# Where the coupling net of the last layer runs: after the attention for half-batches, or by pairs of blocks between other work

## The chip, the cores and the metric

The kernel runs on one core of a Trainium2 chip. A core has a matrix engine (TensorE, PE), a vector engine (VectorE, DVE), an activation engine (ScalarE, ACT), a general engine (GpSimd, POOL) and SyncE (SP), which here only starts DMA transfers. Each engine takes its instructions in a fixed order; they meet through semaphores. TensorE reads SBUF and writes PSUM, which has eight banks of 128 x 512 fp32. The metric is the time of one execution in device microseconds.

## The reference, cut to what matters

Four layers run one after the other over 16 sequences of 256 tokens of 128 features. Each layer adds an attention-like part and a feed-forward part, both of the normalised input. The diff touches the feed-forward part of layer 3 and where it stands:

```python
xn = _layernorm(x)                                  # entering layer 3
x = x + attention(xn, Wq, Wk, Wv, Wo) + ffn(xn)     # causal, 16 heads of 8

def ffn(x):
    gf = global_net(x.mean(axis=1))                 # 128-64-32-1, sigmoid
    out = x
    for _ in range(3):
        tf = coupling_net(out)                      # 128-128-64-32-1, exact gelu, sigmoid
        coupling = 0.1 + adaptive_range * (0.7 * gf + 0.3 * tf - 0.5) * 2.0
        out = out + coupling * twist(out)           # swaps quarters of the features, with signs
    return out
```

Layer 2 adds `attention over a window of 3` and a feed-forward part of `silu(x w1) * (x w2)`, two 512 x 512 products with exact gelu, and a 512 x 128 product.

## The kernel before, in words

The tokens are eight blocks of 512 (two sequences each). `X[i]` holds a block with tokens on partitions, `xT[i]` its normalised form with features on partitions. All products are fp32.

**Layer 2** (L1108 to L1193) goes block by block. `window(i)` makes q, k, v and the windowed softmax, with DVE, ACT and POOL doing most of it; eight products a and b give h0; then 16 products of 128x512 for h1 and 16 for h2 (the loop at L1173), and `po`, the 20 small products that come out with tokens on partitions. A scheduler orders this part by what the program says first. While block i is in h1 and h2, `ahead` normalises block i - 1 for layer 3 through `norm_steps` (L175), which takes a step at each `next`. Eight single PSUM banks are in use (`banks(8, 0)`).

**Layer 3's attention** (`attention`, L800, called at L1223) has its order written out by hand for PE, ACT and DVE (L991). It is a pipeline over sequences s = 0 to 17: for sequence s, `maxima` (three steps of scores `sc` and their DVE maxima M); one sequence later `weights` (three steps of exponents E, with the causal part cut by POOL); two later `context` and `divide`. `project` makes the next block's Q, K, V between steps, `shift` turns the maxima (`mT`) and builds Q2, `turn` makes `cT[i]`. PSUM is held as two single banks and three pairs (`banks(2, 3)`). An iterator `beside` is advanced twice or three times per sequence; in layer 3 it is `means` (L1213): it normalises block 7 and then takes the mean of every sequence (`gx`). Layer 1 calls the same function with hooks in its gaps (`dense(s, gap, cT)`).

**The coupling stage** (L1229 to L1420) follows. For a half of four blocks, `first` is the 128-128 product c1 (per block), `second` the 128-64 product c2 (two blocks side by side in the array), `third` the 64-32 product c3 (four blocks side by side), `fourth` the 32-128 product c4, which repeats the scalar coupling over all 128 partitions, and `twists` the product that swaps quarters. DVE and POOL update `xT`. The two halves alternate over three cycles:

```python
                for cyc in (1, 2):
                    first(0, cyc, range(0, 2))
                    third(1, cyc - 1)
                    first(0, cyc, range(2, 4))
                    fourth(1, cyc - 1)
```

For the last cycle of each half, and all of half 0, a second form is kept with tokens on partitions: `columns_of` (L1277) gets the couplings by tiny products `cd`; `finish_first` (L1339) combines them with the kept normalised blocks `xn3` on POOL and DVE; `turn_second` and `finish_second` (L1366) do the last twist of half 1. `attended` (L1325) multiplies `cT[i]` by Wo and adds it to `X[i]`. The eight output transfers leave from the two finish functions.

Of the kernel before, what the change touches and what calls it, by code (L numbers as in the profile page):

```python
# [9 lines left out]
F32 = mybir.dt.float32  # L10
# [8 lines left out]
P = 128  # L19
B, S, D = 16, 256, 128  # L20
NBLK = 8
# [17 lines left out]
PK3 = dict(wq=256, wk=256, wv=128, wo=128, c1=128, c2=64, c3=32, c4=128, cd=4, g1=64, g2=32, g3=128,  # L39
# [12 lines left out]
def program(ctx: ExitStack, tc: tile.TileContext, x, consts, consts0, rows, pk0, w0s, w0e, pk1, pk1i, pk2, pk3, out):  # L52
# [122 lines left out]
    def norm_steps(pool, blocks, layer, into=None):  # L175


        n = len(blocks) * NT
        mv = pool.tile([P, n, 2], F32, tag="mvs", name=f"mv{layer}_{blocks[0]}")
        for k, i in enumerate(blocks):  # L180
            stats(pool, X[i], mv[:, k * NT : (k + 1) * NT, :], f"st{layer}_{i}")
            yield
        r = inv_std(pool, mv, n, f"r{layer}_{blocks[0]}")
        for k, i in enumerate(blocks):
            t = into(i) if into else pool.tile([P, NT, D], F32, tag="xn", name=f"xn{layer}_{i}")
            normalise(t, X[i], mv, r, k * NT)
            yield
            ps = transpose4(t, f"xnT{layer}_{i}")
            nc.scalar.copy(xT[i], ps)
            yield  # L190
# [609 lines left out]
    def attention(ap_, kp_, blocks, w, layer, beside=iter(()), dense=None, keep=NBLK):  # L800
# [190 lines left out]
        with tc.manual_schedule(engines={mybir.EngineType.PE, mybir.EngineType.Activation, mybir.EngineType.DVE}):  # L991
            for _ in project(blocks[0]):
                pass
            coming = iter(())
            turns = []
            for s in range(len(seqs) + 2):
# [3 lines left out]
                for step in range(3):  # L1000
                    if now:
                        maxima(*now, step)
                    if step < 2:
                        next(beside, None)
                    if step == 0 and old:
                        context(*old)
# [88 lines left out]
    xn3p = ctx.enter_context(tc.tile_pool(name="l3n", bufs=1, side="right"))  # L1095
    xn3 = {}

    def kept(i):

        t = xn3[i] = (xn3p if i in HALVES[0] else fp).tile(  # L1100
            [P, NT, D], F32, tag=f"xn{i}" if i in HALVES[0] else "xn", name=f"xn3_{i}"
        )
        return t


    with banks(8, 0), tc.tile_pool(name="l2w", bufs=1) as wp, tc.tile_pool(name="l2", bufs=2) as sp:
# [47 lines left out]
        ahead = iter(())  # L1154
        for blocks in HALVES:
            norm_half(blocks, 2)
            for i in blocks:

                if i > 0:
                    ahead = norm_steps(fp, (i - 1,), 3, kept)  # L1160
                steps = window(i)
                next(steps)
                h0 = sp.tile([P, 4, 512], F32, tag="h0", name=f"h0_{i}")
# [10 lines left out]
                for wn, sn in (("h1", "t1"), ("h2", "t2")):  # L1174
                    for _ in range(2):
                        next(ahead, None)
                    hn = sp.tile([P, 4, 512], F32, tag=wn, name=f"{wn}_{i}")
                    wv = W2[wn].rearrange("p (c o) -> p c o", c=4)
                    for c in range(4):
                        ps = bank(f"{wn}_{i}_{c}")  # L1180
                        for kc in range(4):
                            mm(ps, wv[:, kc, c * P : (c + 1) * P], prev[:, kc, :], kc == 0, kc == 3)
                        nc.scalar.activation(hn[:, c, :], ps, AF.Gelu, scale=W2[sn][:, c : c + 1])  # L1183
# [14 lines left out]
    with tc.tile_pool(name="l3w", bufs=1) as wp:  # L1198

        hb4 = wp.tile([P, 1], F32, tag="hb4", name="hb4")  # L1200
        nc.vector.tensor_scalar(hb4, W3["cb4"], 0.5, None, ALU.mult)
        hg3 = wp.tile([P, 1], F32, tag="hg3", name="hg3")
        nc.vector.tensor_scalar(hg3, W3["gb3"], 0.5, None, ALU.mult)

        c2 = wp.tile([P, 1], F32, tag="c2", name="c2")
        nc.vector.tensor_scalar(c2, W3["ar"], 0.3, None, ALU.mult)
        ar2 = wp.tile([P, 1], F32, tag="ar2", name="ar2")
        nc.vector.tensor_scalar(ar2, W3["ar"], 2.0, None, ALU.mult)

        with banks(2, 3), tc.tile_pool(name="l3a", bufs=2) as sp:  # L1210
            gx = wp.tile([P, B], F32, tag="gx", name="gx")

            def means():  # L1213
                yield from norm_steps(fp, (NBLK - 1,), 3, kept)
                for i in range(NBLK):
                    nc.vector.tensor_reduce(
                        gx[:, 2 * i : 2 * i + 2], xT[i].rearrange("p (b s) -> p b s", b=2), AX.X, ALU.add
                    )
                    yield
                nc.vector.tensor_scalar(gx, gx, 1.0 / S, None, ALU.mult)  # L1220
                yield

            cTs = attention(sp, wp, range(NBLK), W3, 3, means())  # L1223

        with banks(4, 0), tc.tile_pool(name="l3t", bufs=4, space=PSUM, reuse_waits="tile") as tp, \
                tc.tile_pool(name="l3", bufs=2, reuse_waits="tile") as sp:  # L1229
            base = wp.tile([P, B], F32, tag="base", name="base")  # L1230

            def context_net():
                ps = bank("gc1")
                mm(ps[0:64, 0:B], W3["g1"], gx)
                g1 = sp.tile([64, B], F32, tag="g1", name="g1")
                nc.scalar.activation(g1, ps[0:64, 0:B], AF.Gelu, bias=W3["gb1"][0:64])
                ps = bank("gc2")
                mm(ps[0:32, 0:B], W3["g2"][0:64], g1)
                g2 = sp.tile([32, B], F32, tag="g2", name="g2")
                nc.scalar.activation(g2, ps[0:32, 0:B], AF.Gelu, bias=W3["gb2"][0:32])  # L1240
                ps = bank("gc3")
                mm(ps[:, 0:B], W3["g3"][0:32], g2)
                nc.scalar.activation(base, ps[:, 0:B], AF.Tanh, bias=hg3, scale=0.5)

                nc.vector.tensor_scalar(base, base, 0.35, 0.35 + 0.15 - 0.5, ALU.mult, ALU.add)
                nc.vector.tensor_scalar(base, base, ar2, 0.1, ALU.mult, ALU.add)

            h1, h2, h3, tws, olds = {}, {}, {}, {}, {}


            turn = [None, None]

            def first(hf, cyc, ns):
                for n in ns:
                    i = HALVES[hf][n]
                    ps = bank(f"c1_{i}_{cyc}")
                    mm(ps, W3["c1"], xT[i])
                    h1[i] = sp.tile([P, 512], F32, tag="c1", name=f"c1_{i}_{cyc}", bufs=8)
                    nc.scalar.activation(h1[i], ps, AF.Gelu, bias=W3["cb1"])

            def second(hf, cyc):
                for p in range(2):
                    ps = bank(f"c2_{hf}{p}_{cyc}")
                    for n in range(2):
                        mm(ps[64 * n : 64 * n + 64], W3["c2"], h1[HALVES[hf][2 * p + n]])
                    h2[hf, p] = sp.tile([P, 512], F32, tag="c2", name=f"c2_{hf}{p}_{cyc}", bufs=4)
                    nc.scalar.activation(h2[hf, p], ps, AF.Gelu, bias=W3["cb2"])

            def third(hf, cyc):
                ps = bank(f"c3_{hf}_{cyc}")  # L1270
                for n in range(4):
                    r = slice(64 * (n % 2), 64 * (n % 2) + 64)
                    mm(ps[32 * n : 32 * n + 32], W3["c3"][r], h2[hf, n // 2][r])
                h3[hf] = sp.tile([P, 512], F32, tag="c3", name=f"c3_{hf}_{cyc}", bufs=3)
                nc.scalar.activation(h3[hf], ps, AF.Gelu, bias=W3["cb3"])

            def columns_of(hf, cyc):  # L1277
                ps = bank(f"cd_{hf}_{cyc}")
                for t in range(NT):
                    mm(ps[:, 4 * t : 4 * t + 4], h3[hf][:, t * P : (t + 1) * P], W3["cd"])  # L1280
                c = sp.tile([P, 2, 2, 4], F32, tag="cc", name=f"cc_{hf}_{cyc}", bufs=4)
                nc.scalar.activation(c.rearrange("p b t n -> p (b t n)"), ps[:, 0:16], AF.Tanh, bias=hb4, scale=0.5)
                of = base[:, 8 * hf : 8 * hf + 8].rearrange("p (n b) -> p b n", b=2)
                V = nc.vector
                for b in range(2):
                    V.scalar_tensor_tensor(
                        c[:, b], c[:, b], c2, of[:, b].unsqueeze(1).to_broadcast([P, 2, 4]), ALU.mult, ALU.add
                    )
                if cyc == 0 or hf == 1:
                    turn[hf] = (None, c)  # L1290
                    return
                a, b = (sp.tile([P, 2, 2, 4], F32, tag=k, name=f"{k}_{hf}_{cyc}", bufs=4) for k in "ab")
                pa, pb = turn[hf]
                V.tensor_tensor(a, pb, c, ALU.mult)
                if pa is None:
                    V.tensor_scalar(a, a, -1.0, 1.0, ALU.mult, ALU.add)
                    V.tensor_tensor(b, pb, c, ALU.add)
                else:
                    V.tensor_tensor(a, pa, a, ALU.subtract)
                    V.tensor_tensor(b, pa, c, ALU.mult)  # L1300
                    V.tensor_tensor(b, b, pb, ALU.add)
                turn[hf] = (a, b)

            def twists(hf, cyc):

                for n, i in enumerate(HALVES[hf]):
# [269 lines left out]
```

## Time and profile before

| | us |
|---|---|
| three executions | 1379.95, 1381.39 (median), 1388.58 |
| the profiled execution | 1382.97 |
| its span in the profile | 1381.3 |
| TensorE busy in the span | 1261.4 (91%) |
| VectorE busy | 774.8 (56%) |
| ScalarE busy | 573.5 (42%) |
| GpSimd busy | 349.0 (25%) |
| granted TensorE clock, mean | 0.967 of full |

All times below are from the start of the span. An fp32 product stands in the profile as two passes. A group's line gives source line, engine, operation, out<-in by the program's names, the shape and the count; then busy us, mean ns of one, and the idle time of that engine just before, with what ended it. All products issued through the helper `mm` carry its line L113, so they are told apart by names: h, po, a, b of layer 2; sc, se, av of the attention; c, tw, cd, gc of the coupling stage (c1 is `c<-xT`; c2, c3 and c4 are `c<-c` in 128*64, 64*32 and 32*128).

### The profile page before, as it was taken

What the parts mean: (1) busy time and instruction counts of PE and PEld (TensorE: products, weight loads), DVE (VectorE), ACT (ScalarE), POOL (GpSimd) and SP (SyncE); (2) the same over time, 40 slices, a digit from 0 to 9 for tenths busy, and PEclk for the clock granted to TensorE, in tenths of its full rate; (3) what the DMA queues carried; (4) which work ended last, traced back from release to release, by engine and by line L of the source; (5) the groups of instructions that cost most, each with busy time, mean ns of one, the idle gap of its engine ahead of it and who ended that gap; (6) DMA issues with size and microseconds to landing.
All of it is one profiled execution on the core that took longest, in us unless ns stands there. A gap on an engine that the chain in (4) does not pass through costs nothing.

```text
span 1381.3 us, 27861 instructions
## 1 busy us (share of the span) xinstructions
PE 1261.4 (91%) x11726; PEld 824.8 (60%) x11726; DVE 774.8 (56%) x1567; ACT 573.5 (42%) x896; POOL 349.0 (25%) x510
## 2 busy tenths in 40 slices
PE   3779999979999989999999999999979999988995
PEld 2656899855566566665555554555556666666443
DVE  7565444657767766645345445543367655653464
ACT  4612323334544435434234333443345455543451
POOL 1177104532210000001112211221114434344023
PEclk9789999988999999999999999999999999998998
DMA  7959769740000000000000000000000000000002
GB/s 216 337 180 325 214 173 284 219 170 19 17 6 8 1 2 2 2 1 1 0 0 0 1 1 0 1 0 0 0 2 2 2 2 2 2 2 2 1 0 61
DMA packets 71149, 78.04 MB, mean 56 GB/s; under 512 B 7664, under 2 KB 60400, under 8 KB 70384
## 3 DMA queue, kind: packets, MB, share of 16 engines
q1 hardware_dynamic: 66352, 66.52, 15.7%
q0 software_dynamic: 4240, 8.99, 2.0%
q8 instruction: 93, 1.52, 0.5%
q10 hardware_dynamic: 432, 0.75, 0.2%
q14 instruction: 32, 0.26, 0.1%
HBM read 55.59 MB, written 20.64 MB: 55 GB/s over the span
## 4 chain that ended last, share of the span: by engine, by line
PE 78%; DVE 13%; ACT 5%; issue 2%; POOL 2%; DMA 1%; POOLq 0%; DVEq 0%; ACTq 0%
PE h L113 16%; PE sc L113 8%; PE se L113 7%; PE po L113 6%; PE av L113 5%; DVE M L897 4%; PE c L113 3%; PE sy L113 3%; PE sg L113 3%; PE su L113 3%; PE mT L912 3%; PE pq L113 2%; ACT E L941 2%; PE a L113 2%; PE b L113 2%
## 5 line engine op out<-in xcount | busy, mean ns | idle before, releaser
L897 DVE TENSOR_REDUCE M<-sc 128x4 f32<-128x1024 f32 (+3 forms) x256 | 195.9, 818 | 66.1 <-PE sc L113 66.0
L113 PE MATMUL h<-h,pk 128*128 128x512 f32 x512 | 224.2, 596 | 2.6 <-DVE h L1169 2.6
L941 ACT ACTIVATE E<-se 128x1024 f32<-128x1024 f32 (+1 forms) x192 | 158.8, 879 | 85.6 <-PE se L113 85.2
L113 PEld LDWEIGHTS h<-h,pk 128*128 128x128 f32 x512 | 97.2, 191 | 119.8 <-issue 112.1
L948 POOL TENSOR_SCALAR_AFFINE_SELECT E<-E 64x256 f32<-64x256 f32 x256 | 106.0, 414 | 155.5 <-ACT E L941 144.1
L113 PE MATMUL se<-Q,Km 32*128 32x256 f32 (+3 forms) x2048 | 123.0, 339 | 15.9 <-DVE M L897 14.4
L113 PEld LDWEIGHTS sc<-Kp,Qm 32*128 32x128 f32 x2048 | 93.2, 191 | 58.7 <-issue 28.9
L113 PE MATMUL sc<-Kp,Qm 32*128 32x192 f32 (+3 forms) x2048 | 122.8, 335 | 4.8 <-ACT E L941 3.0
L113 PEld LDWEIGHTS se<-Q,Km 32*128 32x128 f32 x2048 | 88.8, 190 | 53.9 <-issue 36.0
L609 POOL DMA_INDIRECT yk<-YS,slots x64 | 61.4, 959 | 182.6 <-DVE x L619 88.1
L1183 ACT ACTIVATE h<-h,pk 128x512 f32<-128x512 f32 x64 | 43.9, 687 | 141.8 <-PE h L113 141.7
L119 POOL TENSOR_TENSOR v_r<-mv,power 128x4 f32<-128x4 f32 (+2 forms) x17 | 4.0, 235 | 350.7 <-DVE mv L140 350.6
L1193 DVE TENSOR_TENSOR x<-x,po 128x512 f32<-128x512 f32 x8 | 5.5, 686 | 141.0 <-PE po L113 141.0
L395 POOL DMA_INDIRECT XS<-xn,slots x64 | 65.4, 1021 | 73.0 <-DVE slots L374 53.7
L113 PE MATMUL av<-E,vals 128*32 128x256 f32 (+3 forms) x2048 | 77.5, 301 | 3.4 <-POOL E L948 2.0
L966 ACT COPY cu<-av 128x512 f32<-128x512 f32 x32 | 18.7, 585 | 144.8 <-PE av L113 144.8
L113 PEld LDWEIGHTS av<-E,vals 128*32 128x32 f32 x2048 | 52.6, 110 | 24.3 <-POOL E L948 3.1
L591 DVE TENSOR_TENSOR hs<-hs,su 128x512 f32<-128x512 f32 x46 | 31.6, 687 | 57.4 <-PE su L113 57.3
L1127 POOL TENSOR_TENSOR pr<-q,k 128x512 f32<-128x512 f32 (+2 forms) x24 | 28.2, 1205 | 127.5 <-ACT k L1120 127.5
L835 DVE TENSOR_SCALAR Km<-Kp,consts 128x512 f32<-128x512 f32 x64 | 33.2, 560 | 45.3 <-ACT Kp L833 45.3
L144 DVE TENSOR_SCALAR xn<-x,mv,r 128x128 f32<-128x128 f32 x100 | 47.4, 535 | 18.6 <-POOL r L120 18.6
L113 PE MATMUL pk<-xT,pk 128*128 128x512 f32 x80 | 46.7, 671 | 6.7 <-ACT Qm L828 6.7
(276 smaller groups left out, 2259.8 us busy)
## 6 DMA issues: line engine op xcount, KB each, us to landing
we<-in_w0e SPq DMA_DIRECT2D x46, 384.0 KB, 4.4
toe<-kd SPq DMA_DIRECT2D x32, 512.0 KB, 7.8
xs<-XS SPq DMA_DIRECT2D x46, 128.0 KB, 3.5
YS<-ys SPq DMA_DIRECT2D x46, 128.0 KB, 3.0
XS<-Z SPq DMA_DIRECT2D x4, 1024.0 KB, 7.6
pk<-in_pk SPq DMA_DIRECT2D x1, 3145.5 KB
x<-in_x SPq DMA_DIRECT2D x8, 256.0 KB, 6.9
ycd<-yc SPq DMA_DIRECT2D x8, 256.0 KB, 6.7
```

What stands on the lines that cost most here:

```text
L113: nc.tensor.matmul(o, l, r, start=start, stop=stop)
L144: nc.vector.tensor_scalar(dst[:, t, :], src[:, t, :], mv[:, at + t, 0:1], r[:, at + t : at + t + 1], ALU.subtract, ALU.mult,)
L395: d = nc.gpsimd.indirect_dma_start(out=XS[hf][:, :], out_offset=at_rows(slots[:, hf, k, n : n + 1]), in_=xn[HALVES[hf][n // NT]][:, n % NT ...
L591: nc.vector.tensor_tensor(h, h, pu, ALU.mult)
L609: nc.gpsimd.indirect_dma_start(out=y, out_offset=None, in_=YS[hf][:, :], in_offset=at_rows(slots[:, hf, k, n : n + 1]),)
L835: nc.vector.tensor_scalar(t["Km"][:, T, :, j, :], chunks(t["Kp"][:, T, :]), C["hmask"][:, j : j + 1], C["hone"][:, j : j + 1], ALU.mult, A ...
L897: nc.vector.tensor_reduce(dst, src, AX.X, ALU.max, negate=True)
L912: nc.tensor.transpose(ps[:, T, c * P : (c + 1) * P], negm[bl][:, c, T].rearrange("p g j k -> p (g j k)"), ident)
L941: nc.scalar.activation(E[:, 2 * n : 2 * n + 2, :], se[n][:, :, 0 : 2 * wide], AF.Exp, scale=ISQ)
L948: nc.gpsimd.affine_select(out=d[r], in_=d[r], pattern=[[0, 2], [0, 2], [1, 64]], compare_op=ALU.is_ge, fill=0.0, base=0, channel_multiplie ...
L1127: nc.gpsimd.tensor_tensor(pr[:, :, j:], q[:, :, j:], k[:, :, 0 : S - j], ALU.mult)
L1183: nc.scalar.activation(hn[:, c, :], ps, AF.Gelu, scale=W2[sn][:, c : c + 1])
```

## The change

The coupling net becomes a generator over a pair of blocks, `coupling(p, keep)`, of 15 steps: c1, c2, c3, c4 and twist in each of three cycles. The context net (gc1 to gc3) runs inside the first cycle for the pair's four sequences. All three cycles use the form with features on partitions; the token form, `xn3`, the constant `cd`, and all GpSimd work of the stage are gone. A pair's c3 is two tiles side by side where the old one was four.

Pair 0 (blocks 0, 1) starts in layer 2's block 3 and goes on in block 4, pair 1 in blocks 5 and 6; one step stands after each of the eight h1 and h2 products of 128 rows of output. Pair 2 is in block 7, with a step after every half of such a product. Pair 3 is in the first sequence (s = 0) of layer 3's attention, two steps in each of its eight gaps. Block 7's normalisation for layer 3 stands whole between the first projection and the first scores. The output product of block i, now with the coupled block added by a product with the identity, its add on DVE and its transfer stand in gap 2 of sequence 2i + 5; that of block 7 after the loop. h0, h1 and h2 share four buffers in place of two each. `norm_steps` computes the inverse root one step earlier.

```diff
@@ norm_steps
             stats(pool, X[i], mv[:, k * NT : (k + 1) * NT, :], f"st{layer}_{i}")
+            if i == blocks[-1]:
+                r = inv_std(pool, mv, n, f"r{layer}_{blocks[0]}")
             yield
-        r = inv_std(pool, mv, n, f"r{layer}_{blocks[0]}")
@@ attention
+            for _ in early:
+                pass
...
+                    if dense and step == 0:
+                        dense(s, -1, cT)
@@ before layer 2
+    def coupling(p, keep):
+        two = (2 * p, 2 * p + 1)
...
+        for cyc in range(3):
+            x = xT if cyc == 0 else coupled
+            h1 = []
+            for i in two:
+                ps = bank(f"c1_{i}_{cyc}")
+                mm(ps, W3["c1"], x[i])
+                h1.append(np_.tile([P, 512], F32, tag="c1", name=f"c1_{i}_{cyc}", bufs=2))
+                nc.scalar.activation(h1[-1], ps, AF.Gelu, bias=W3["cb1"])
...
+            yield
+            ps = bank(f"c2_{p}_{cyc}")
+            for n in range(2):
+                mm(ps[64 * n : 64 * n + 64], W3["c2"], h1[n])
...
+            yield
+            ps = bank(f"c3_{p}_{cyc}")
+            for n in range(2):
+                r = slice(64 * n, 64 * n + 64)
+                mm(ps[32 * n : 32 * n + 32], W3["c3"][r], h2[r])
...
+            yield
+            cs = []
+            for n, i in enumerate(two):
+                r = slice(32 * n, 32 * n + 32)
+                ps = bank(f"c4_{i}_{cyc}")
+                mm(ps, W3["c4"][r], h3[r])
+                c = np_.tile([P, 2, S], F32, tag="c4", name=f"c4_{i}_{cyc}", bufs=2)
+                nc.scalar.activation(c.rearrange("p b s -> p (b s)"), ps, AF.Tanh, bias=hb4, scale=0.5)
+                cs.append(c)
...
+            yield
+            for n, i in enumerate(two):
+                c = cs[n]
+                ps = bank(f"tw_{i}_{cyc}")
+                mm(ps, C["twist"], x[i])
+                for b in range(2):
+                    k = 2 * n + b
+                    nc.vector.tensor_scalar(c[:, b], c[:, b], c2, base[:, k : k + 1], ALU.mult, ALU.add)
+                c = c.rearrange("p b s -> p (b s)")
+                nc.vector.tensor_tensor(c, c, ps, ALU.mult)
...
+                nc.vector.tensor_tensor(y, x[i], c, ALU.add)
+                coupled[i] = y
+            yield
@@ layer 2
+                if i in (3, 5, 7):
+                    net = coupling((i - 3) // 2, np_)
...
-                h0 = sp.tile([P, 4, 512], F32, tag="h0", name=f"h0_{i}")
+                h0 = sp.tile([P, 4, 512], F32, tag="hid", name=f"h0_{i}", bufs=4)
...
                         for kc in range(4):
                             mm(ps, wv[:, kc, c * P : (c + 1) * P], prev[:, kc, :], kc == 0, kc == 3)
+                            if kc == 3 or kc == 1 and i == NBLK - 1:
+                                next(net, None)
@@ layer 3 (means, context_net, first ... finish_second and their order go)
+    with banks(2, 3), tc.tile_pool(name="l3w", bufs=1) as wp, tc.tile_pool(name="l3a", bufs=2) as sp:
+        net = coupling(NBLK // 2 - 1, wp)
+        def output(i, cT):
+            po = bank(f"po3_{i}")
+            for t in range(NT):
+                ts_ = slice(t * P, (t + 1) * P)
+                mm(po[:, ts_], cT[i][:, ts_], W3["wo"], True, False)
+                mm(po[:, ts_], coupled[i][:, ts_], ident, False, True)
+            xf = X[i].rearrange("p t d -> p (t d)")
+            nc.vector.tensor_tensor(xf, xf, po, ALU.add)
+            nc.sync.dma_start(out=ov[i], in_=X[i])
+        def between(s, gap, cT):
+            if s == 0:
+                for _ in range(2):
+                    next(net, None)
+            if gap == 2 and s % 2 == 1 and s >= 5:
+                output((s - 5) // 2, cT)
+            if s == 2 * NBLK + 2:
+                output(NBLK - 1, cT)
+        attention(sp, wp, range(NBLK), W3, 3, dense=between, early=norm_steps(fp, (NBLK - 1,), 3))
```

## The prediction

> **What bounds the kernel now.** I first cut the span into stages and read how much of each TensorE fills. Columns are the stretch and its length, then busy us (and count) of PE, PE's weight loads, DVE, ACT and POOL, then the granted clock:
>
> ```profile
> 640.60:1002.50 361.90, 359.09 (x1146) 189.68 (x1145) 166.32 (x268) 137.09 (x188) 71.82 (x64) 1.00 0.00 1
> 1002.50:1022.60 20.10, 14.67 (x137) 8.67 (x135) 12.20 (x29) 9.12 (x16) 1.21 (x2) 0.92 0.01 2
> 1022.60:1237.00 214.40, 200.65 (x3173) 138.24 (x3172) 134.83 (x220) 114.23 (x164) 87.53 (x212) 1.00 0.01 2
> 1237.00:1281.60 44.60, 35.84 (x511) 26.17 (x509) 16.92 (x30) 16.30 (x23) 18.46 (x45) 0.81 0.01 2
> 1281.60:1366.00 84.40, 82.44 (x390) 41.15 (x390) 45.07 (x88) 40.96 (x67) 17.11 (x20) 1.00 0.01 4
> 1366.00:1381.30 15.30, 0.00 (x0) 0.00 (x0) 8.24 (x23) 0.27 (x1) 5.81 (x9) 0.55 0.41 120
> ```
>
> They are layer 2, the first sequence of layer 3's attention, its steady sequences, its last ones, the coupling stage, and the drain. Layer 2, into which three quarters of the net move, has 2.8 us of idle TensorE in 362. The stage they leave has 2 us in 84; only its drain, 15.3 us, is free of PE. So the move hides no PE work where it goes: it saves the drain and the start, and whatever gets dearer is paid in full.
>
> Is a busy PE there at its peak? The groups by line show 512 passes of h in 224.2 us, 0.44 each, though one takes 596 ns:
>
> ```profile
> L113 PE MATMUL h<-h,pk 128*128 128x512 f32 x512 | 224.2, 596 | 2.6 <-DVE h L1169 2.6
> ```
>
> An fp32 product of 128x512 is two such passes, 0.86 us, back to back: there is no slack behind the records. Next, the timeline of the coupling stage prices its products (start, us, what, passes):
>
> ```profile
> 1296.31 1.88 PE L113 MATMUL c<-xT,pk 128*128 128x512 f32 x4
> 1298.12 1.06 PE L113 MATMUL c<-c,pk 64*32 64x512 f32 x8
> 1299.11 1.98 PE L113 MATMUL c<-xT,pk 128*128 128x512 f32 x4
> 1285.42 1.98 PE L113 MATMUL c<-xT,pk 128*128 128x512 f32 x4
> 1286.58 0.69 ACT L1259 ACTIVATE c<-c,pk 128x512 f32<-128x512 f32 x1 [0.78 <-PE c L113]
> ```
>
> Two c1 products last from 1296.31 to 1298.12, 1.81 us where four passes at 0.43 make 1.72. The c3 of four blocks, four tiles side by side, lasts to 1299.11: 0.99 for two rounds of 0.43. The last two lines give a hop: the Gelu starts 1.16 after its product's start, 0.30 after its 0.86 of issue; with 0.69 of Gelu and 0.15 to the next product, PE without other work stands 1.15.
>
> **Layer 2 gains pairs 0 to 2.** A pair's cycle is c1 twice and twist twice (4 x 0.86 = 3.44) and c2, c3 and c4, each two rounds with two tiles side by side. The rule that speaks against it is in the Trainium skill, TensorEngine Tiling (Array Packing), Key Properties: a change of tiling mode drains the engine. It names no price. The rows do: 0.09 on entering and 0.13 on leaving (1.81 against 1.72, 0.99 against 0.86). Between h products every tiled step pays both, so 3 x (0.86 + 0.22) = 3.24, and a cycle is 6.68. Nine cycles are 60.1; with free changes they would be 54. A c3 per pair costs what one per four blocks did, and the third cycle now runs c4 and twist for all blocks. The three tiny products of the context net stood at 0.23 to 0.39; at 0.35 they are 3.2 for three pairs.
>
> Waits: mostly an h product of 3.43 lies between two steps, more than the hop, so Gelus and adds cost nothing (uncovered, each is 1.15). In blocks 4 and 6 the cover fails. VectorE's reciprocal ends 11.35 after the first h1 product starts (880.96 in this block):
>
> ```profile
> 880.96 13.90 PE L113 MATMUL h<-h,pk 128*128 128x512 f32 x32
> 888.97 3.34 DVE L1149 RECIPROCAL den<-den 128x512 f32<-128x512 f32 x1
> ```
>
> The instruction order puts the second cycle's scaling behind it: seven operations of 0.3 to 0.7 (a 128x512 scale takes 0.56, a product 0.69), so the first y comes at 14.6, when c1 of cycle 3 is due at 13.1; the second y adds 0.5. That is 2.0 a block, and h1's last products queue behind it: 4. In block 7 steps stand only half a product apart: c2, due 5.15 after h1's start, waits for Exps (to 3.5), a table load of 1.28 and two Gelus: 1.1. Sum 60.1 + 3.2 + 5.1 = 68; ends 62 and 75.
>
> **First sequence.** It takes the last pair: 3 x 6.68 less the c1/twist restarts, plus the context net, 20.3 us of PE. Here nothing lies beside it but the sequence's own scores. Block 7's normalisation, formerly beside the scores, now stands ahead: DVE works on Km until 1009.99, then statistics 1.25, POOL 1.34 and the first normalise, so the transpose and the scores queued behind it start 4.6 later. Hops I count with the order at hand: in cycle 1, c1-c2 1.05, c2-c3 0.7, c3-c4 and its net 1.9, the second twist 1.15 (two PSUM banks only; its bank waits for three Q copies), the second y 0.9; in cycle 2, 1.85, 1.05, 1.05, 0.75; in cycle 3, 3 x 1.05. With the 1.6 that stay from pk, PE stands about 19, against 5.4 in the row above. So +13.6 of standing and +20.3 of work make 34, and DVE reaches sequence 1's maxima 2.7 late, since eight operations of the last twist stand before them; the exponent's second score pair waits for those maxima. 36.5.
>
> Clock: the Trainium skill, TensorE: Matmul & The Clock Gate, HAM oscillation, says that gaps over some 3.4 us cost the clock. By it only the 4.6 us gap counts, about 2 us. The rows are harsher:
>
> ```profile
> 1251.50:1254.90 3.40, 2.28 (x40) 1.59 (x36) 0.57 (x1) 1.94 (x2) 1.65 (x4) 1.00 0.00 0
> 1254.90:1258.30 3.40, 2.53 (x29) 2.12 (x30) 1.92 (x4) 0.31 (x1) 0.00 (x0) 0.51 0.02 5
> ```
>
> PE was busy 2.28 of 3.40 us, no gap of that length, and got half the clock next. The new sequence is about 0.6 busy in many such stretches; 1.3 us for each that drops, none to six of them: 0 to 8. I take 3.5, so 40 in all; ends 26 and 50.
>
> **Outputs.** Each is 16 passes of 128x128; the old stage issued 64 (four blocks) in 7.25, so 1.81. Seven fall into sequences, before an exponent's scores:
>
> ```profile
> 1125.63 0.44 PE L113 MATMUL se<-Q,Km 32*128 32x64 f32 x4
> 1126.91 0.45 PE L113 MATMUL se<-Q,Km 32*128 32x64 f32 x4 [0.85 <-DVE M L897]
> ```
>
> PE stands 0.85 there, so six cost 1.0 each, 6 us (0 to 11 by how much is absorbed). The DVE add of 0.69 goes before the reciprocal, where DVE had 0.52 to spare. Stores move onto SP between sequences: 256 KB land in 2.3 us, on a queue with nothing else. The means (eight of 0.68) leave DVE; sequences with and without them took 15.7 to 16.2 alike: 0.
>
> **What goes.** From the last cT copy's end, 1281.53, to 1381.30 are 99.8. In their place: the seventh output before the last context turn, 1.25 after the 0.69 that PE stood there; then 1.9 PE, 0.3, 0.7 add and 3.5 from there to the end, as the last x write (1377.88) shows: 7.6. Net -92; ends -93 and -90.
>
> **Nothing.** Up to block 3's first h product the two orders agree on every engine save four constants of 0.15 (beside po) and mean reductions, so the earlier inverse root changes neither queue nor wait; a gain is excluded for the same reason. Four shared hidden buffers for six: the tile reused was read a block earlier. One ACT table load of 1.28 goes, inside the 99.8.
>
> **Sum.** 68 + 40 + 6 - 92 = +22. The profiled execution took 1382.97 with a span of 1381.3, 1.6 above the median 1381.39; I add to the median: 1403. One per cent, 14 us, is about what a measurement of this kernel tells from no change.
>
> **Rivals.** First, not slower: the hops in the first sequence are covered. Place: between its maxima, where ACT and DVE were 9.1 and 12.2 of 20.1 busy. If they run ahead, it grows only by 20.3, with layer 2 at 64 without waits and the outputs at 4: 64 + 20 + 4 - 92 = -4, 1377. It decides when the sequence grows less than 24. For it speaks the free time of ACT and DVE; against it PE's fixed order and two banks. Chance 0.22, spread 1365 to 1395; 0.04 of it is faster by over 1%. Second, worse: the clock is lost through most of the first sequence (50) and in layer 2's 2 us waits, and VectorE's queue delays h0: 75 + 50 + 9 - 91 = +43, 1424. Chance 0.16. That the change isn't made as it says is excluded by the instruction order. My case has 0.62, mostly 1394 to 1413. The range that leaves out a tenth on either side is 1385 to 1420. Slower 0.76, same 0.20, faster 0.04.
>
> **What would show it.** Layer 2 at 424 to 437 us, still PE-filled, with PE waiting for DVE's y in blocks 4 and 6; the first sequence about 60 us with some 20 of standing and clock rows under 1; odd sequences 1 longer; after the last cT copy 6 to 7. Wrong if the tiled steps slip in without the change cost (layer 2 under 420) or the first sequence stays under 44.

## The result, and the profile after

The changed kernel takes 1404.08 us (median of four, 1401.85 to 1405.73) against 1380.67 for the kernel before on the same chip (four, 1379.21 to 1388.58): 23.4 us more, ratio 1.016 with a 95% interval of 1.012 to 1.020. Predicted were 1403.0, range 1385 to 1420, slower by over 1% with chance 0.76. The profiled execution took 1401.85, its span is 1400.2.

The stages of the changed kernel, columns as in the prediction's first view (stretch, length, busy of PE, its weight loads, DVE, ACT, POOL, granted clock):

```profile
634.60:1066.30 431.70, 426.05 (x1351) 209.86 (x1351) 208.04 (x354) 174.87 (x252) 71.86 (x64) 1.00 0.00 1
1066.30:1125.90 59.60, 46.55 (x200) 17.99 (x198) 23.37 (x52) 23.45 (x39) 1.21 (x2) 0.80 0.00 1
1125.90:1349.00 223.10, 210.89 (x3255) 148.13 (x3254) 135.59 (x223) 112.46 (x162) 87.43 (x212) 0.98 0.03 8
1349.00:1394.00 45.00, 37.20 (x542) 27.62 (x540) 17.99 (x32) 16.26 (x22) 18.39 (x45) 0.89 0.05 13
1394.00:1400.20 6.20, 2.05 (x16) 1.86 (x16) 0.69 (x1) 0.00 (x0) 0.00 (x0) 1.00 0.16 46
```

Layer 2 is 431.7 us long and still full of TensorE. The first sequence, up to the second one's scores, is 59.6, with PE idle for 13 and the clock at 0.80. The coupling stage and its drain are gone; 6.2 us remain behind the last cT copy.

For the account I cut both traces at the same instructions: layer 3's first query product (1002.57 before, 1066.28 after), the transposes of the second sequence's maxima (1036.52, 1144.79), the end of the last cT copy (1281.54, 1393.96). From layer 2's first query product on:

| | before | after | difference | predicted |
|---|---|---|---|---|
| layer 2 | 363.6 | 431.7 | +68.1 | +68 |
| query product to second sequence's maxima turned | 33.95 | 78.51 | +44.6 | +40 |
| from there to the last cT copy | 245.0 | 249.2 | +4.2 | +6, and 1.25 counted in the tail |
| after the last cT copy | 99.8 | 6.2 | -93.5 | -93.4 |
| sum | | | +23.3 | +22 |

The spans differ by 18.9 only, since layer 2 began 4.4 earlier in this one profiled execution; ahead of it TensorE runs the same 6373 passes in both kernels, and only four small constants and the place of an inverse root differ. The 23.3 is what the medians show too.

The second stretch, which the experiments come back to, before and after:

```profile
1002.57:1036.52 33.95, 26.23 (x310) 16.35 (x309) 22.82 (x45) 16.93 (x26) 5.62 (x13) 0.95 0.01 2
1066.28:1144.79 78.51, 61.33 (x377) 27.45 (x375) 35.60 (x72) 29.37 (x47) 5.50 (x13) 0.80 0.00 1
```

TensorE is busy 35.1 us longer there, for 67 passes more; it stands 17.2 in place of 7.7, and its granted clock falls from 0.95 to 0.80.

The h group of layer 2 and the new tiled rows, from the groups by line in that stretch (count, busy us, mean ns, idle just before):

```profile
L113 PE MATMUL h<-h,pk 128*128 128x512 f32 x512 | 230.9, 597 | 2.7 <-DVE h L1252 2.7
L113 PE MATMUL c<-y,pk 128*128 128x512 f32 x24 | 11.9, 606 | 2.6 <-DVE y L1181 2.6
L113 PE MATMUL c<-c,pk 128*64 128x512 f32 x36 | 10.3, 618 | 0.3 <-ACT c L1121 0.3
L113 PE MATMUL c<-c,pk 32*128 32x512 f32 x36 | 10.1, 640 | 0.0
L113 PE MATMUL c<-c,pk 64*32 64x512 f32 x36 | 9.4, 601 | 0.0
```

The 512 passes of h, 224.2 us before, fill 230.9. No pass is longer (597 ns against 596); what grew is the time around them. The waits are small: 2.6 us for y, 0.3 for c2's Gelu.

Block 4's timeline shows the wait that was forecast there (start, length, engine, operation, idle before and what ended it):

```profile
851.19 3.34 DVE L1229 RECIPROCAL den<-den 128x512 f32<-128x512 f32 x1
...
856.85 0.68 DVE L1181 TENSOR_TENSOR y<-y,c 128x512 f32<-128x512 f32 x1
857.45 0.67 DVE L1176 TENSOR_TENSOR c<-c,tw 128x512 f32<-128x512 f32 x1
857.68 1.10 PE L113 MATMUL c<-y,pk 128*128 128x512 f32 x2 [1.06 <-DVE y L1181]
858.16 0.69 DVE L1181 TENSOR_TENSOR y<-y,c 128x512 f32<-128x512 f32 x1
859.00 1.10 PE L113 MATMUL c<-y,pk 128*128 128x512 f32 x2 [0.23 <-DVE y L1181]
```

The reciprocal ends 11.35 after h1's start (843.18), and c1 of the third cycle waits 1.06 and 0.23 for the sums behind it.

The first sequence and the start of the second in windows of 3.4 us:

```profile
1073.10:1076.50 3.40, 0.00 (x0) 0.00 (x0) 2.01 (x10) 1.16 (x2) 1.09 (x2) 1.00 0.00 0
1076.50:1079.90 3.40, 2.76 (x20) 1.95 (x20) 1.11 (x4) 0.58 (x1) 0.11 (x1) 0.50 0.03 7
1079.90:1083.30 3.40, 3.40 (x12) 1.31 (x8) 2.63 (x3) 0.62 (x1) 0.00 (x0) 0.50 0.00 0
1083.30:1086.70 3.40, 2.62 (x10) 0.53 (x10) 1.08 (x3) 1.59 (x4) 0.00 (x0) 1.00 0.00 0
1086.70:1090.10 3.40, 2.18 (x10) 0.65 (x6) 0.00 (x0) 1.40 (x3) 0.00 (x0) 1.00 0.00 0
1090.10:1093.50 3.40, 3.23 (x5) 1.67 (x6) 1.14 (x4) 1.50 (x5) 0.00 (x0) 0.51 0.00 0
1093.50:1096.90 3.40, 2.62 (x4) 0.84 (x3) 2.02 (x4) 1.21 (x3) 0.00 (x0) 0.50 0.00 0
1096.90:1100.30 3.40, 3.40 (x5) 0.84 (x3) 1.38 (x2) 0.69 (x1) 0.00 (x0) 0.50 0.00 0
...
1110.50:1113.90 3.40, 3.40 (x24) 1.37 (x22) 2.93 (x6) 0.00 (x0) 0.00 (x0) 0.52 0.00 0
...
1120.70:1124.10 3.40, 3.40 (x13) 2.00 (x13) 0.00 (x0) 1.78 (x3) 0.00 (x0) 0.53 0.03 7
...
1130.90:1134.30 3.40, 3.16 (x14) 1.69 (x14) 1.32 (x2) 1.85 (x2) 0.69 (x2) 0.53 0.00 0
1134.30:1137.70 3.40, 3.40 (x38) 2.36 (x36) 1.00 (x2) 0.67 (x2) 0.97 (x3) 0.50 0.00 0
```

The first row is block 7's normalisation: no product for a whole window, then two windows at half clock. The next drop follows a window that was filled to 2.18 of 3.40, with no gap of that length. In these rows a "busy" PE is a slow PE: five passes fill 3.23 us, where at full clock one follows the other after 0.43. The twist products of the first cycle, here and in layer 2 at full clock (mean of a pass 1101 and 592 ns), show the same:

```profile
L113 PE MATMUL tw<-xT,consts 128*128 128x512 f32 x4 | 4.0, 1101 | 0.8 <-DVE c L1176 0.8
L113 PE MATMUL tw<-xT,consts 128*128 128x512 f32 x12 | 5.6, 592 | 0.0
```

Nine of the 23 windows of this stretch stood at 0.50 to 0.53, with TensorE busy 28.8 us in them; in the kernel before it was one of ten, with 3.0. If half of that busy time is the clock's doing, the change lost (28.8 - 3.0) / 2 = 12.9 us to it, an estimate; of the 35.1 us, 22.2 are then left for the products.

In the second sequence, VectorE comes late to the maxima:

```profile
1131.14 2.08 PE L113 MATMUL se<-Q,Km 32*128 32x256 f32 x12 [3.21 <-DVE M L898]
```

The row it answers to, in the kernel before, waits 0.68:

```profile
1025.37 1.13 PE L113 MATMUL se<-Q,Km 32*128 32x256 f32 x12 [0.68 <-DVE M L897]
```

### The profile page after: what moved, and what is told of

It is laid out like the page before. It is cut to its first block, busy times and chain, and to the rows that moved or that the text cites. A ratio compares the mean times of both kernels' runs of the same rounds, so it can differ in the third digit from the quotient of the medians.

```text
span 1400.2 us, 27879 instructions
## 1 busy us (share of the span) xinstructions
PE 1282.3 (92%) x11728; PEld 819.4 (59%) x11728; DVE 774.2 (55%) x1572; ACT 581.3 (42%) x912; POOL 323.6 (23%) x482
## 4 chain that ended last, share of the span: by engine, by line
PE 75%; DVE 12%; ACT 5%; issue 3%; DMA 2%; POOL 2%; SPq 0%; POOLq 0%; DVEq 0%; ACTq 0%
PE h L113 14%; PE sc L113 9%; PE se L113 7%; PE po L113 6%; PE av L113 5%; PE c L113 4%; DVE M L898 3%; PE mT L913 3%; PE pq L113 2%; PE pk L113 2%; PE sg L113 2%; PE sy L113 2%; PE su L113 2%; ACT E L942 2%; PE a L113 2%
## 5 line engine op out<-in xcount | busy, mean ns | idle before, releaser
L113 PE MATMUL h<-h,pk 128*128 128x512 f32 x512 | 230.9, 597 | 2.7 <-DVE h L1252 2.7
L942 ACT ACTIVATE E<-se 128x1024 f32<-128x1024 f32 (+1 forms) x192 | 158.8, 879 | 94.0 <-PE se L113 93.4
L396 POOL DMA_INDIRECT XS<-xn,slots x64 | 63.0, 985 | 69.9 <-DMA toe<-kd 50.7
```

What stands on the lines that cost most here:

```text
L113: nc.tensor.matmul(o, l, r, start=start, stop=stop)
L396: d = nc.gpsimd.indirect_dma_start(out=XS[hf][:, :], out_offset=at_rows(slots[:, hf, k, n : n + 1]), in_=xn[HALVES[hf][n // NT]][:, n % NT ...
L942: nc.scalar.activation(E[:, 2 * n : 2 * n + 2, :], se[n][:, :, 0 : 2 * wide], AF.Exp, scale=ISQ)
```

## The experiments

Each was timed beside the kernel before. In the set of E5 to E8 every kernel took about 100 us longer, the kernel before too (1484.55): in their traces layer 2 begins 96 to 107 us later, for a cause that is not known and lies ahead of what the edits touch. So those are compared by differences and by stages. "The section" is the stretch from layer 3's first query product to the second sequence's turned maxima, 33.95 us before and 78.51 after.

**E1: no pair in the first sequence.**

```diff
-        net = coupling(NBLK // 2 - 1, wp)
+        net = iter(())
+        coupled.update({6: xT[6], 7: xT[7]})
```

> The changed kernel without the coupling of blocks 6 and 7 in the first sequence of layer 3's attention (their outputs take the uncoupled values); block 7's normalisation still stands ahead. In the changed kernel, from the first query product of layer 3 to the exponent transposes of the second sequence, 78.5 us pass, in the kernel before 33.95. My theory (the pair costs its 20 us of products, plus standing, plus the half clock that the standing brings): 38 to 40 us here, so 39 us come off, and the time is about 1365 (1362 to 1369). Rival (the hops are covered and only the pair's products count): 20 us come off, 58 here, 1384.

1362.14 us against 1379.20 before (0.984 to 0.988), so 40.5 below the changed kernel's +23.4; the section takes 39.3. The pair costs 39 us there, twice its products: the rival of covered hops falls.

```profile
1068.79:1108.07 39.28, 30.84 (x310) 17.36 (x309) 21.57 (x43) 16.91 (x26) 5.50 (x13) 0.83 0.00 1
```

5.3 us are left over the kernel before. With the same 310 passes TensorE is busy 4.6 longer, at 0.83 of the clock for 0.95, and stands only 0.7 longer: it waits 4.1 for block 7's normalisation, but less elsewhere.

**E2: no normalisation of block 7.**

```diff
-        attention(sp, wp, range(NBLK), W3, 3, dense=between, early=norm_steps(fp, (NBLK - 1,), 3))
+        attention(sp, wp, range(NBLK), W3, 3, dense=between)
```

> The changed kernel without the third layer's normalisation of block 7 (its transposed values stay those of layer 2's normalisation), everything else as it was. The prediction priced the normalisation ahead of the scores at 4.6 us. In the trace of the changed kernel TensorE stands idle through a whole 3.4 us window there, and the two windows after it run at half clock; so my theory now: 4.1 us of standing go, and with them about 3 us of half clock, together 6 to 8, time 1396 to 1398, granted clock 1.0 in the windows that follow. Rival (only the standing goes, the clock falls at the next hop anyway): 4 to 5, time 1399 to 1400. Second rival (the pair's own first hop takes the wait over): under 2.

1392.78 against 1379.20 (1.007 to 1.012), 9.8 below the changed kernel's difference and so more than the 6 to 8 expected; by stages the section falls by 10.2:

```profile
1067.91:1136.26 68.35, 54.05 (x372) 23.79 (x371) 33.04 (x60) 28.70 (x46) 4.29 (x11) 0.90 0.00 1
```

Standing shrinks by only 2.9 (17.2 to 14.3); the other 7.3 are busy time, of which the four transposes left out took 1.2 in the changed kernel. The wait of 4.1 was worth more than double its length. And a wait appears that the changed kernel did not have in this section: c1 for y, 1.2 us. With the clock at 0.90 for 0.80, PE is early enough to wait.

**E3: the pair spread over two sequences**, one step in each gap.

```diff
-            if s == 0:
-                for _ in range(2):
-                    next(net, None)
+            if s < 2:
+                next(net, None)
```

> The changed kernel with one step of the last pair in each gap of the first two sequences instead of two in each gap of the first: the same products, but other scores between any two steps; three Gelu steps then fall among Exps, each with two table loads of 1.28 us on ScalarE. From layer 3's first query product to the exponent transposes of the second sequence: 78.5 in the changed kernel. Theory (standing 17.2 there and about 14 us lost to half clock are the hops' doing): 60 to 66, time 1387 to 1392. Rival (work-bound: 61.3 us of TensorE busy stay busy): 75 to 79, time 1400 to 1404. Second rival (the table loads come onto the path): 70 to 75, time 1396 to 1400.

1391.09 against 1379.20 (1.005 to 1.011). The section takes 66.4, a little above the 60 to 66 of the theory, the time is within it:

```profile
1068.75:1135.16 66.41, 55.28 (x377) 24.29 (x376) 34.17 (x69) 35.52 (x53) 8.15 (x17) 0.89 0.00 1
```

The same products, 6 us less of busy and 6 less of standing. Of the gaps that remain, 4.1 is the normalisation. ScalarE is busy 29.4 in the changed kernel and 35.5 here, with the table loads; PE's waits for it sum to 7.1, against 8.8 in the changed kernel, so the loads did not lengthen them.

**E4: idle products in the waits.** Three before block 7's transposes, one before each c2, c3 and c4 of the last pair; the last are overwritten by the real product.

```diff
+    def idle(p, ps):
+        if p == NBLK // 2 - 1:
+            mm(ps, W3["c1"], xT[0])
...
             ps = bank(f"c2_{p}_{cyc}")
+            idle(p, ps)
```

> The changed kernel with twelve idle products of 128x128x512 (0.86 us each at full clock, 10.3 in all, results overwritten or unread) put where TensorE stands in the first sequence: three before block 7's transposes, one before each c2, c3 and c4 of the last pair. They change only how busy TensorE is. Theory now (half clock costs about 13 us from layer 3's first query product to the second sequence's exponent transposes, far more than the 3.5 of the prediction): the granted clock there rises from 0.80 to over 0.9, and 78.5 us become 68 to 74, time 1394 to 1400, although work is added. Rival (the prediction's 3.5 us of clock, the rest standing): the fillers are hidden in the standing and gain no more than 3: 76 to 80, time 1402 to 1406. If neither the standing nor the clock holds: up to 10 longer.

1400.07 against 1379.20 (1.012 to 1.017), at the edge of the expected time; the section, which the theory spoke of, takes 73.9 (68 to 74 expected):

```profile
1068.93:1142.87 73.94, 61.03 (x401) 26.19 (x399) 35.60 (x72) 29.38 (x47) 5.50 (x13) 0.95 0.00 1
```

TensorE is busy 61.0 us as in the changed kernel (61.3), but 10.3 of it are the idle products: the kernel's own take 50.7. So at least 10.6 us of the changed kernel's busy time there were half clock, brought back by nothing but work that nobody needs; at 0.95 the clock is not whole yet, and the 12.9 of the windows fits. 4.3 of the idle products lay in standing, the rest was paid. By the whole time the gain is 2.5 (20.9 above the kernel before, for 23.4), which is not clear of noise; it is shown for the section. The waits for y come up here too (1.8), for the same reason as in E2.

**E5: c2, c3 and c4 without tiles**, one full product each with as many passes.

```diff
-            for n in range(2):
-                mm(ps[64 * n : 64 * n + 64], W3["c2"], h1[n])
+            mm(ps, W3["c1"], h1[0])
...
-                r = slice(32 * n, 32 * n + 32)
-                ps = bank(f"c4_{i}_{cyc}")
-                mm(ps, W3["c4"][r], h3[r])
+                if n == 0:
+                    ps = bank(f"c4_{i}_{cyc}")
+                    mm(ps, W3["c4"], h3)
```

> The changed kernel with c2, c3 and c4 of every pair as one full product of 128x128x512 each, in place of two tiles side by side (so another net is computed, and of the pair's second block only c1, twist and the two last sums remain; as many passes of 0.43 us, none of them tiled). Layer 2, from its first query product to that of layer 3, takes 431.7 us in the changed kernel, 363.6 before. Theory of the prediction (0.22 us for each tiled step, 27 of them there): 425.8 (425 to 427). Rival (the change of mode is free, and the 6.7 us by which the h group grew are only gaps around any foreign product): 431 to 432. If the change costs more than 0.22, up to 422. The whole time goes down by that and by about 2 us in the first sequence: 1394 to 1397 by the theory.

Layer 2 takes 425.92 in place of 431.72, 5.8 less for 27 steps, 0.215 each, where the rows of the kernel before had given 0.22. That is the net price: its waits for y are 3.4, where the changed kernel's were 2.6, so a step by itself cost 0.24. The edit takes the tiles and the changes of mode away together; no run tells them apart. Its groups:

```profile
L113 PE MATMUL h<-h,pk 128*128 128x512 f32 x512 | 229.6, 594 | 2.7 <-DVE h L1249 2.7
L113 PE MATMUL c<-c,pk 128*128 128x512 f32 x54 | 27.7, 594 | 0.3 <-ACT c L1121 0.3
L113 PE MATMUL c<-y,pk 128*128 128x512 f32 x24 | 11.9, 605 | 3.4 <-DVE y L1178 3.4
```

The h group hardly shrinks (230.9 to 229.6), so its growth was mostly not the change of mode: a pass is recorded with 0.597 us where the next follows after 0.43, so at every break in a run of h the group keeps 0.17 more, and some 40 breaks by the 45 steps make the 6.7. The rival read the h group rightly and the total wrongly. The total is the measure. The whole time is 5.8 above the kernel before, so 17.6 below the changed kernel's difference, more than the 7 to 10 expected: the section gained 7.9 (70.6) and not 2, at a clock of 0.90, and 3.9 are in no stage that I compared.

**E6: the spread pair, with the three idle products before block 7's transposes** (E3 and the first part of E4).

> The spread pair (one step in each gap of the first two sequences, which took 66.4 us from the first query product to the second sequence's exponent transposes) with three idle products of 0.86 us, results unread, before block 7's transposes, where TensorE stood 4.1 us and then lost half its clock for two windows of 3.4 us. Theory (half clock follows the empty window): these two windows come back at full clock, 63 to 64 us, time 1387 to 1389. Rival (the clock is lost at another place instead): 66 to 67, time 1390 to 1392.

```profile
1168.46:1230.44 61.98, 53.57 (x382) 23.25 (x381) 33.41 (x67) 34.59 (x52) 6.61 (x14) 0.97 0.00 1
```

The section falls from 66.4 to 62.0, below the 63 to 64 of the theory, the clock is 0.97. The time is 4.7 us above the kernel before (1.001 to 1.004), 7.2 less than in E3. Later in the same trace one sequence takes 17.74 where it took 16.16 in E3: a drop of the clock in another place took 1.6 back.

**E7: the kernel before with idle products** in the last block's gaps, where no projection is left.

```diff
+                elif now and now[1] == 0 and late:
+                    coming = idle()
...
+            def idle():
+                for n in range(6):
+                    mm(bank(f"idle_{n}"), w["wq"][:, 0:P], xT[blocks[0]])
+                    yield
```

> The kernel before with one idle product of 128x128x512 (0.86 us, result unread) in each gap of the last block's two sequences of layer 3, where otherwise the next block's projections stand; nothing else is changed. These two sequences take 17.65 and 17.22 us against 15.8 and 16.15 of those with projections, and windows at half clock follow those that TensorE filled to 0.61 and 0.66. Theory (half clock makes the difference): both fall to 15.8 to 16.3, the granted clock of the attention's end goes up from 0.81 to over 0.9, time 2 to 4 us shorter. Rival (the idle products are work like any other): sequences of 18 to 20 us, time 2 to 5 us longer.

The two sequences take 15.79 and 15.36 in place of 17.65 and 17.22. The second of them in the kernel before and in this one:

```profile
1245.72:1262.94 17.22, 15.06 (x217) 11.28 (x217) 8.81 (x14) 5.68 (x8) 6.61 (x16) 0.77 0.01 2
```

```profile
1343.78:1359.14 15.36, 15.00 (x222) 9.72 (x223) 8.72 (x14) 5.15 (x8) 6.64 (x17) 1.00 0.01 2
```

TensorE gets more work and is busy no longer. The time is 2.05 us below the kernel before (0.996 to 0.999): at the edge of the expected 2 to 4, and less than the 3.7 of the two sequences. In the profiled execution the second sequence took 20.07, against 16.65 in the profile of the kernel before, with the same instructions; windows at half clock fell into it. That execution was still one of the faster of its set (1478.17, median 1482.50), so this one trace does not explain the median.

**E8 and E10: what can be had without the change.** Both keep the coupling stage. They add E7's idle products, put the attention part of the first seven outputs (eight passes each) into the attention's gaps, let TensorE mask the last sequence, and divide the drain differently: in E8 VectorE turns blocks 1 and 3 as GpSimd turns the others; in E10 it forms the first term of all four blocks with fused multiply-adds, and the quarters of block 1.

```diff
+            masks = late and (i, bl) != (blocks[-1], 1)
...
+            def between(s, gap, cT):
+                if gap == 2 and s % 2 == 1 and s >= 5:
+                    output((s - 5) // 2, cT)
...
-                    nc.gpsimd.tensor_tensor(y, y, wide(a, D), ALU.mult)
-                    nc.vector.tensor_tensor(x, x, y, ALU.add)
+                    for t in range(NT):
+                        nc.vector.scalar_tensor_tensor(
+                            x[:, t], y[:, t], col(a, n)[:, t : t + 1], x[:, t], ALU.mult, ALU.add)
```

> The kernel before, its coupling stage kept, with what the trace and the runs so far say of single parts: the idle products of the run above; the attention part of the first seven outputs (eight passes each, 0.9 us in the coupling stage) in the attention's gaps, where the full outputs of the changed kernel cost 0.71 each; the last sequence's masks by TensorE in place of the 5.5 us chain of selections on GpSimd that it waits for; and the turn of blocks 1 and 3 in the drain on VectorE in place of GpSimd. Expected: 2.5 by the idle products, 6.3 less six times 0.3 to 0.7 by the outputs, 2 to 3 by the masks, 5 to 6 by the drain: 12 to 15 us, time 1365 to 1368. Rival (the drain stays, since VectorE is as late as GpSimd, and the coupling stage stands in the place of the removed outputs): 1372 to 1376.

E8: 1468.13 against 1484.55, 16.4 less (0.985 to 0.991). By its trace 11.5 come off from layer 3's first product to the end (378.7 to 367.2): 6.1 in the attention, 2.95 of them by the masks, and 5.4 behind the last cT copy. The first five outputs cost nothing in the gaps (odd sequences 16.15, as before), the sixth 0.6 (15.97, against 15.36 in E7). The drain gave 2.7, not 5 to 6, in part since a product with a broadcast factor takes VectorE 1.49 us where I had reckoned 0.69; and the coupling stage gave 2.7 where 6.3 of products had gone; its clock was 0.96, for 1.00 before.

> The kernel before with the same two edits at its attention's end, the attention part of the first seven outputs in the attention's gaps, and another division of the drain: GpSimd forms only the quarters of blocks 0, 2 and 3, VectorE those of block 1 and, with four fused multiply-adds of 0.26 each per block, the first term of all (a whole product with a broadcast factor took VectorE 1.49 in the last such kernel, not 0.69). The last such kernel took 11.5 us less than before by the stages of its trace, from layer 3's first query product to the end (378.7 to 367.2). Expected: VectorE done with the first half after 9 us in place of 11.9, so 364 to 365.5 for that stretch, and 13 to 17 us against the kernel before on the same chip. Rival (the drain hangs on the last columns, not on VectorE): 367, 11 to 12 us.

E10: 1366.32 against 1381.34, 15.0 less (0.988 to 0.991); 37.8 below the changed kernel's median. Its attention, and its stage with the drain:

```profile
1001.19:1274.10 272.91, 257.18 (x3896) 177.57 (x3895) 167.40 (x285) 139.60 (x202) 100.61 (x242) 0.99 0.01 2
1274.10:1364.90 90.80, 77.22 (x333) 35.09 (x331) 53.77 (x122) 41.16 (x68) 15.12 (x20) 0.93 0.08 24
```

In the kernel before these stretches take 278.97 and 99.76; the sum here is 363.7, just under the 364 to 365.5 expected.

**E9: the change with all of it**: spread, idle products before block 7's transposes and at the end, masks by TensorE.

> The changed kernel with all that the runs found against its first sequence, and with what helped the kernel before at its end: the last pair spread over two sequences, three idle products before block 7's transposes, idle products in the gaps of the last block's sequences, the last sequence's masks by TensorE. By the stages measured so far: 1404.1 less 12.1 (spread) less 4.4 (idle products there) less 2.5 (the end's idle products) less 2.9 (masks) = 1382, so 0 to +4 us against the kernel before on the same chip: the change would then be worth nothing, but cost nothing. Rival (what is mended at one place is lost as half clock at another): +8 to +14 against before.

1385.82 against 1381.34 (1.001 to 1.005): 18.9 of the 23.4 are gone, 16.5 of them in the section, and 4.5 stay, just outside the expected 0 to 4.

```profile
1065.43:1127.41 61.98, 53.71 (x383) 23.27 (x382) 33.40 (x67) 34.60 (x52) 6.61 (x14) 0.97 0.00 1
1127.41:1373.87 246.46, 236.59 (x3641) 166.26 (x3639) 144.25 (x239) 122.35 (x176) 94.37 (x228) 0.99 0.03 9
1373.87:1380.10 6.23, 2.05 (x16) 1.86 (x16) 0.69 (x1) 0.00 (x0) 0.00 (x0) 0.94 0.15 43
```

The attention's end gave 2.7 of the 5.4 hoped for, and one sequence took 17.78 for 16.16 at half clock, as in E6. So the change's loss lay mainly in where the last pair stood, but even with that mended it gains nothing: what the three pairs pay in layer 2 and the fourth in the attention is a little more than the stage and its drain had cost.

## Why the prediction was right, and where its terms were not

The account of layer 2 and of the end held, and they make most of the sum. That the first sequence came so near is in good part luck: its terms erred in opposite directions.

**Layer 2, +68, was right in sum and nearly in its parts.** TensorE's busy time there rose by 65.3 (63.3 predicted: 60.1 and the context net's 3.2), its idle time by 2.8 (5.1 predicted). By block the growth is 11.2 and 11.8 for pair 0, 11.2 and 11.8 for pair 1, 22.3 for pair 2. E5 gives the net price of the tiled steps, 0.215 for the 0.22. The waits were over-sized: the second-cycle sums came when the prediction said (the first y at 857.53, 14.35 after h1's start; 14.6 predicted), but c1 was due later, 13.44 instead of 13.1, and the wait was 1.06 + 0.23, not 2.0; its "h1's last products queue behind it" happened at that size. Block 7's c2 waited 0.3, not 1.1. That the work was 2 dearer and the waits 2.3 cheaper is partly one thing: a step that takes longer leaves less to wait for, as the waits of E5, longer with cheaper steps, show.

**The first sequence, +40, was +44.6, and its terms were wrong both ways.** The term that failed is the clock: "none to six of them: 0 to 8. I take 3.5". Nine windows fell; by them it is 12.9, an estimate, and E4 alone brought back 10.6. Standing, with the late maxima, was put at 13.6 + 2.7 = 16.3 (its single hops add up to 19.8 and not 19, so 0.7 more was due even by my own list); it grew by 9.5 (7.7 to 17.2), and the "some 20 of standing" in the first sequence were 13. The rest, 22.2 of busy time, stands against 20.3 of products. So the clock was 9.4 too low, the products 1.9 too low and the standing 6.8 too high. The errors are not independent: at half clock products stretch over the hops, so that waits vanish, and they come back when the clock does (the waits for y in E2 and E4). I had added hops at full clock and a small sum for lost clock, where one replaces the other. The rule that I had weighed, in the Trainium skill, TensorE: Matmul & The Clock Gate, HAM oscillation (gaps over some 3.4 us), gave 2 and was the farthest off: it fits the one empty window, and misses the drop behind the window filled to 2.18. The next section of the same page, "A second HAM failure mode: psum-queue depth-cycling", tells of a clock that oscillates because TensorE idles briefly and often between groups of products, there from cycling through PSUM banks. The nine windows at half clock here, among waits of 0.6 to 1.4 us for Gelus and the like, look the same, and I had not weighed it.

**Block 7's normalisation, 4.6,** was 4.1 as a wait and 10.2 with what hung on it (E2).

**The late maxima.** Predicted 2.7 behind the last twist; the wait for them is 3.2 where it was 0.7, 2.5 more.

**Outputs, 6 x 1.0.** Sequences 5, 7, 9, 11 and 13 took 16.87 for 16.16: 0.71 each. The output covers somewhat more than the wait of 0.85: from the start of the exponent's scores to the next product it is 1.31 (1203.86 to 1205.17) in place of 2.58 (1125.63 to 1128.21), and a wait of 0.18 for the Exps comes new. The seventh output lengthens the last stretch by 1.7 (1.25 predicted), and 1.2 came back by clock in the sequence ahead of it.

**The tail, -92 with the seventh output,** held almost to the number: 99.8 gone, 6.2 in its place against 6.4.

**The rivals.** "Hops covered" is excluded by E1: the pair costs 39, not 20. "Clock lost" was half right: the mechanism was there and its first-sequence number, 50, was missed by 5 on one side as mine by 5 on the other; but layer 2 kept its full clock throughout (1.00), and its waits did not reach 75.

What stays open: what exactly drops the clock. Over layer 3's attention in all twelve traces, of the windows of 3.4 us at full clock those filled to 0.64 or more nearly all kept it (all but 12 of 1033) and most of those under 0.63 lost it (24 of 40), but one of the changed kernel with 1.78 of 3.40 (from 1103.7) kept it, and ones filled to 0.74 (E3) and 0.76 (E9) lost it. So by these traces the filling of one window does not decide alone.

## What to carry to other kernels

Work moved to a place where TensorE is full cost its whole length plus what it paid to fit in, here 0.2 us for each tiled step; the gain is only what had no TensorE work at the old place. Look first whether the old place can be bettered where it is: E10 took 15 us off, 9 of them behind the last cT copy, while the move lost 23. A chain of short dependent products with little beside it cost twice over, once in waits and once in clock: spreading its steps helped most (12 us of the section), products in the waits less (4.4 to 4.6), and clock and standing are to be reckoned together, since less of the one brought back some of the other. When a sum agrees with the measured time, look at its terms: two of mine were wrong by 9 and 7 in opposite directions.

## What the hardware showed that I had not expected

Products without use made stretches shorter: 10.3 us of them shortened one by 4.6 (E4), and six in two sequences took 3.7 us off these (E7), where the whole kernel became faster too, by 2. The granted clock was 1.00 or 0.50 in nearly every window. The same instructions took 16.65 and 20.07 us in two profiles, by where the half-clock windows fell, and a gain at one place was partly lost at another that was not touched (17.74 for 16.16, E6, E9); a stage's time has such a spread even where the instructions and the data are the same.
